# ScalarE and VectorE in source order: an attention and quantised-convolution kernel with its instruction order tied down on two engines

## Chip, cores and metric

The kernel runs on one core of one Trainium2 chip. The metric is the device time of one execution in microseconds (us). Five engines work side by side: TensorE (PE; its weight loads are PEld), ScalarE (ACT), VectorE (DVE), GpSimd (POOL) and SyncE (SP, which here only issues DMAs).

## What is computed

Input `x` is 16 images of 128 channels by 1024 pixels (32 x 32), all float32. First an attention layer with four heads, then two 3x3 convolutions on 4-bit activations with batch statistics. Cut to what matters:

```python
qkv = einsum('bchw,oc->bohw', x, w_qkv) + b_qkv            # 4 heads, 128 channels each
scores = einsum('bnc,bcm->bnm', q, k) * c ** -0.5           # 1024 x 1024 per image and head
out = einsum('bnm,bmc->bnc', softmax(scores), v)
x = einsum('bchw,oc->bohw', out, w_out) + b_out + x
# second layer: act_quant = round(15 * clip(x, 0, 1)) / 15, weights to 4 bits as well
out = conv3x3(act_quant(x), weight_quant(w1));  out = batchnorm(out, gamma1, beta1)
out = conv3x3(act_quant(out), weight_quant(w2)); out = batchnorm(out, gamma2, beta2)
return out + x
```

## The kernel before

Nearly all of the time is spent in one loop of `fast_path`. It goes over 63 of the 64 pairs of image and head (`heads`, index `g`; four heads, h = 0 to 3, belong to an image) and, inside a head, over `NK` = 4 steps `k`. The 64th pair (`LAST`) is done by a loop of its own (`score_unit`, `attend_unit`, `normalise_group`), which also starts the first convolution of the last image. The second convolution and the output follow in a second block that the change doesn't touch.

One step does this:

- `scores(g, k)`: TensorE makes four score chunks of 128 x 512, each as two instructions of 64 output rows (`halves`), which go to two halves of the array. I call these halves lanes. The chunks go to three PSUM buffers (`ps_s`, 3), so the fourth chunk of a step has to wait until the first has been read. ScalarE reads each chunk with an exponential into tile `e` (line 551). VectorE then forms the combinations that a Strassen-like scheme with seven products in place of eight needs: lines 554, 555 and 558 (the last one writes T4), and adds them into the running softmax sums `es` (562 in step 1, 564 in steps 2 and 3).
- `run(step, 0)`: work that was registered with `at` for the first half of the step.
- `attend(...)` of the step before: the seven products, each on one lane, into four PSUM banks `psa` (pool `ps_a`, one buffer each). In even steps four of the seven are on the first lane, in odd steps on the second. In an odd step the first product reads T4, and the last goes to bank 0.
- `run(step, 1)`: work registered for the second half.

The registered work of head `g` falls into the next head: `sum_up` (line 625) in its step 0, first half; `evacuate` (595, four copies of `psa` to SBUF on ScalarE) in step 0, second half; `combine` parts 0, 1 and 2 in step 1 (both halves) and step 2 (first half), which pass the result between ScalarE copies that move data to other partitions (605, 606, 607, 612, 615) and VectorE adds (608, 613, 617, 618); `normalise` in step 2, second half, which inverts the sums in a chain of small operations (652 to 660), spreads them (664) and applies them (673, or 675 and 676, and for the last head of an image also 679). With the last head of an image, `quantize` (255 on ScalarE, 256 and 257 on VectorE) and `sums_range` (348, 349) come in the first head of the next image, step 3; `transform_rows` (782) in the second head, step 0; `rows_product` (matmuls `psw`, ScalarE line 798) in steps 2 and 3 and the step after; `rows_output` (805, 806, 808) and `first_statistics` (298) in the third head, steps 0 and 1. The projections `project_u` (matmuls `psu`, ScalarE 509) for the next head come in steps 1 and 2, and `project_v` for the next image (matmuls `psv`, ScalarE copy 530, VectorE 532 and 533) in the last head of an image and the first of the next.

TensorE's order is written out by hand: `product` ties every matmul to the one before with `tc.issue_after`. The other engines' order is left to the scheduler of the framework. It takes the instructions in the order of the source as a priority, but puts one ahead of another where it reckons that the other would still be waiting. `tc.issue_after(x)` adds an edge of order without a semaphore: an instruction is placed behind `x` on its engine. Each engine then executes its own list.

```python
with tc.issue_after(pe[0]) if pe else nullcontext():
    done = nc.tensor.matmul(out_, lhsT=lhsT, rhs=rhs, start=start, stop=stop)
pe[:] = [done.ins]
```

Of the kernel before, what the change touches and what calls it, by code (L numbers as in the profile page):

```python
# [16 lines left out]
NH = 4  # L17
# [174 lines left out]
def fast_path(  # L192
# [29 lines left out]

    outer = ExitStack()
# [24 lines left out]
    def quantize(b, src, scale, bias, r0=0, r1=H):  # L248

        cut = slice(r0 * W, r1 * W)  # L250
        t = qtp.tile([P, (r1 - r0) * W], F32, tag="qt", name="qt")
        if b == B - 1 and scale == A_LEVELS and r1 == H:
            nc.vector.tensor_scalar(t, src[:, cut], scale, 0.0, ALU.mult, ALU.max)
        else:
            nc.scalar.activation(t, src[:, cut], AF.Relu, bias=bias, scale=scale)
        nc.vector.tensor_scalar(t, t, A_LEVELS, MAGIC, ALU.min, ALU.add)
        return nc.vector.tensor_scalar(
            pads[b % NPAD][:, r0 + 1 : r1 + 1, 1 : W + 1],
            t.rearrange("p (h w) -> p h w", w=W),
            MAGIC,  # L260
            None,
            ALU.subtract,
        )
# [82 lines left out]
    def sums_range(b):  # L346
        flat = sums[:, b * NH : (b + 1) * NH, :].rearrange("p g k -> p (g k)")
        nc.vector.tensor_reduce(ext[:, 0, b : b + 1], flat, AX.X, ALU.min)
        nc.vector.tensor_reduce(ext[:, 1, b : b + 1], flat, AX.X, ALU.max)
# [23 lines left out]
    with ExitStack() as ph:  # L373
# [86 lines left out]
        def fold_a(h):  # L460
            wq_h, wk_h, bq_h = wqk_sb[:, h, 0:P], wqk_sb[:, h, P : 2 * P], wqk_sb[:, h, 2 * P :]
            if h == 0:

                ps = ps_m.tile([P, P], F32, tag="mm", name=f"ps_a_{h}")
                bias = ps_a.tile([P, 1], F32, tag="a1", name="ps_a_bias")
            else:
                ps = ps_s.tile([P, P + 1], F32, tag="s", name=f"ps_a_{h}")
                bias = ps[:, P:]
            product(ps[:, 0:P], wq_h, wk_h)
            product(bias, wk_h, bq_h)  # L470
            nc.vector.tensor_scalar(at_sb[:, h, :], ps[:, 0:P], qscale, None, ALU.mult)
            nc.vector.tensor_scalar(au_sb[:, h : h + 1], bias, qscale, None, ALU.mult)

        def fold_b():
            ps = ps_m.tile([P, NH, P], F32, tag="mm", name="ps_b")
            for h in range(NH):
                product(ps[:, h, :], wvo_sb[:, h, 0:P], wvo_sb[:, h, P : 2 * P])
            nc.scalar.copy(bt_sb[:, 1, 1:], ps)
            nc.vector.tensor_copy(bt_sb[:, 1, 0], ps[:, NH - 1])
            nc.scalar.copy(bt_sb[:, 0, :, TOP], bt_sb[:, 1, :, TOP])  # L480
            nc.vector.tensor_tensor(
                bt_sb[:, 0, 0:NH, BOTTOM], bt_sb[:, 1, 0:NH, BOTTOM], bt_sb[:, 1, 0:NH, TOP], ALU.subtract
            )
            nc.vector.tensor_copy(bt_sb[:, 0, NH, BOTTOM], bt_sb[:, 1, NH, BOTTOM])

        def fold_bo():
            ps = ps_s.tile([P, 1], F32, tag="s", name="ps_bo")
            for h in range(NH):
                product(
                    ps,  # L490
                    wvo_sb[:, h, P : 2 * P],
                    wvo_sb[:, h, 2 * P :],
                    start=(h == 0),
                    stop=(h == NH - 1),
                )
            nc.vector.tensor_tensor(bo2_sb, ps, bo_sb, ALU.add)

        def project_u(g, hf, ps=None):
            b, h = heads[g]
            if hf == 0:  # L500
                us[g] = up.tile([P, N], F32, tag="u", name=f"u_{g}")
            if ps is None:
                ps = ps_m.tile([P, HALF], F32, tag="mm", name=f"psu_{g}_{hf}")
            halves(ps, lambda t: at_sb[:, h, LANES[t]], xt[b][:, ts(hf, HALF)])
            dst = us[g][:, ts(hf, HALF)]
            if g == 0 and hf == 0:
                nc.vector.tensor_scalar(dst, ps, au_sb[:, h : h + 1], None, ALU.add)
            else:
                copied = nc.scalar.activation(dst, ps, AF.Identity, bias=au_sb[:, h : h + 1])  # L509
                if g == 0:  # L510
                    load_rest(copied.ins)
# [8 lines left out]
        def project_v(b, k, c, ps=None):  # L520
# [9 lines left out]
            nc.scalar.copy(v[:, c : c + 3 : 2], ps.rearrange("p (h a o) -> p a h o", a=2, o=PH))  # L530
            if c == 1:
                nc.vector.tensor_tensor(v[:, S2], v[:, S3], v[:, A22], ALU.subtract)
                nc.vector.tensor_tensor(
                    v[:, S1 : S4 + 1],
                    v[:, A11 : A12 + 1],
                    v[:, S2 : S2 + 1].to_broadcast([P, 2, NH, PH]),
                    ALU.add,
                )
# [4 lines left out]
        def scores(g, k, between=None):  # L543
# [4 lines left out]
            for i, (c, m) in enumerate(((0, 1), (1, 1), (0, 0), (1, 0))):  # L548
                ps = ps_s.tile([P, HALF], F32, tag="s", name=f"pss_{g}_{k}_{i}")
                score(ps, b, g, k + NK * c, ts(m, HALF))  # L550
                exps[:] = [nc.scalar.activation(e[:, 2 * c + 1 - m], ps, AF.Exp).ins]  # L551
                if between and i in between:
                    between[i]()
            nc.vector.tensor_tensor(e[:, T3], e[:, B12], e[:, B22], ALU.add)  # L554
            nc.vector.tensor_tensor(  # L555
                e[:, T1 : T2 + 1 : T2 - T1], e[:, B12 : B11 + 1], e[:, B11 : T3 + 1 : T3 - B11], ALU.subtract
            )
            nc.vector.tensor_tensor(e[:, T4], e[:, T2], e[:, B21], ALU.add)  # L558
            mine = e[:, T4 : T3 + 1]
            if k == 1:  # L560
                sides[g] = esp.tile([P, NHF, HALF], F32, tag="es", name=f"es_{g}")
                nc.vector.tensor_tensor(sides[g], es[g, 0][:, T4 : T3 + 1], mine, ALU.add)  # L562
            elif k > 1:
                added = nc.vector.tensor_tensor(sides[g], sides[g], mine, ALU.add)  # L564
                sums_added[:] = [added.ins]
# [26 lines left out]
        def evacuate(g):  # L592
            evs[g] = [evp.tile([P, HALF], F32, tag=f"s{i}", name=f"ev_{g}_{i}") for i in range(4)]
            for to, ps in zip(evs[g], psa.pop(g)):
                nc.scalar.copy(to, ps)  # L595
# [5 lines left out]
        def combine(g, part):  # L601
            sa, sb, s3, sd = evs[g]
            if part == 0:
                y = avs[g, "y"] = evp.tile([P, HALF], F32, tag="y", name=f"y_{g}")
                nc.scalar.copy(y[TOP], s3[BOTTOM])
                nc.scalar.copy(y[BOTTOM], sd[TOP])  # L606
                nc.scalar.copy(sd[TOP], sd[BOTTOM])
                nc.vector.tensor_tensor(y, sa, y, ALU.add)  # L608
                return
            y = avs[g, "y"]  # L610
            if part == 1:
                nc.scalar.copy(s3[BOTTOM], y[TOP])
                nc.vector.tensor_tensor(y, y, s3, ALU.add)
            elif part == 2:
                nc.scalar.copy(sa[BOTTOM], y[BOTTOM])
                avs[g] = avp.tile([P, N], F32, tag="av", name=f"av_{g}")
                nc.vector.tensor_tensor(avs[g][:, HALF:], y, sd, ALU.add)
                nc.vector.tensor_tensor(avs[g][:, 0:HALF], sa, sb, ALU.add)
                evs.pop(g), avs.pop((g, "y"))

        def quadrant_sums(total):
# [3 lines left out]
            nc.vector.tensor_reduce(  # L625
# [11 lines left out]
        def inverse_sums(g, part, cut):  # L637
# [3 lines left out]
            if g == LAST:  # L641
# [5 lines left out]
                nc.vector.reciprocal(rinv, ps)  # L647
            else:

                side = smp.tile([Q, P // Q, n], F32, tag="side", name=f"side_{g}")  # L650
                for a in range(P // Q):
                    nc.vector.tensor_copy(side[:, a, :], part[ts(a, Q), :])
                total = smp.tile([Q, n], F32, tag="total", name=f"total_{g}")
                nc.vector.tensor_reduce(total, side.rearrange("p a k -> p k a"), AX.X, ALU.add)

                first, second = total[:, 0 : n // 2], total[:, n // 2 :]
                nc.vector.tensor_tensor(first, first, second, ALU.add)
                nc.vector.reciprocal(rinv[0:Q, :], total)
                for a in range(1, P // Q):
                    nc.vector.tensor_copy(rinv[ts(a, Q), :], rinv[0:Q, :])  # L660
# [3 lines left out]
            nc.vector.transpose(rb, rinv.unsqueeze(2).to_broadcast([P, n, Q]))  # L664
            return rb

        def normalise(g):
# [3 lines left out]
            if h == 0:  # L671
                accs[b] = accp.tile([P, N], F32, tag="acc", name=f"acc_{b}")
                nc.vector.tensor_tensor(accs[b], av, rb, ALU.mult)
                return
            nc.vector.tensor_tensor(av, av, rb, ALU.mult)  # L675
            nc.vector.tensor_tensor(accs[b], accs[b], av, ALU.add)
            if h == NH - 1 or g == LAST - 1:

                nc.vector.scalar_tensor_tensor(accs[b], accs[b], bo2_sb, xt[b], ALU.add, ALU.add)
# [15 lines left out]
        def score_unit(u):  # L695
# [9 lines left out]
            exps[:] = [nc.scalar.activation(e, ps, AF.Exp).ins]  # L705

        def attend_unit(u):
# [8 lines left out]
            elif u == FIRST_UNIT[i] + 1:  # L716
# [6 lines left out]
                nc.vector.tensor_tensor(totals[i], units[(u - 1) // 4][:, (u - 1) % 4], e, ALU.add)  # L723
            else:
                nc.vector.tensor_tensor(total, total, e, ALU.add)
# [15 lines left out]
            elif u + 1 == FIRST_UNIT[i + 1]:  # L741
# [3 lines left out]
                nc.scalar.copy(avs[LAST, i], psa[LAST, i])  # L745
                sides[LAST, i] = quadrant_sums(total)

        def normalise_group(i):
# [4 lines left out]
            nc.vector.tensor_tensor(rb, avs.pop((LAST, i)), rb, ALU.mult)  # L753
            nc.vector.tensor_tensor(x1[:, cut], x1[:, cut], rb, ALU.add)
# [15 lines left out]
        def transform_weights():  # L770
            with tc.issue_after(sums_added[0]):
                nc.vector.tensor_tensor(middle1[:, 1], taps1[:, 0], taps1[:, 2], ALU.add)
                nc.vector.tensor_tensor(middle1[:, 0], middle1[:, 1], taps1[:, 1], ALU.add)
                nc.vector.tensor_tensor(middle1[:, 1], middle1[:, 1], taps1[:, 1], ALU.subtract)

        def transform_rows(b):
# [3 lines left out]
            for k in (1, 2, 0, 3):  # L780
                x_, y_, op = FOUR[k]
                nc.vector.tensor_tensor(works[b][:, k], pick(x_), pick(y_), op)

        def rows_product(b, k):
# [13 lines left out]
            nc.scalar.mul(ms[b, inner][:, k // 2], ps, (1.0, 0.5, 0.5, -1.0)[k])  # L798

        def rows_output(b):  # L800
# [4 lines left out]
            nc.vector.tensor_tensor(both[:, 0], inner[:, 0], inner[:, 1], ALU.add)  # L805
            nc.vector.tensor_tensor(both[:, 1], inner[:, 0], inner[:, 1], ALU.subtract)
            y = ys[b].rearrange("p (i r w) -> p r i w", r=2, w=W)
            nc.vector.tensor_tensor(y, others, both, ALU.add)
# [541 lines left out]
```

## Time and profile before

| | |
|---|---|
| Time, median of 2 runs | 2024.68 us (2022.66 to 2026.7) |
| The profiled execution's own time | 2024.57 us |
| Its span in the profile | 2022.7 us, so 1.9 us lie around it |
| Mean granted TensorE clock | 0.993 |
| PE, DVE, ACT busy | 1987.6, 1722.2 and 1198.5 us |
| DMA | 22 GB/s in the mean |

The span is one profiled execution. A group line gives source line, engine, operation, output and input tiles, count, busy time, mean length of one, and the idle time of the engine just before, with what ended it. Times of a timeline are microseconds from the start of the span. A float32 matmul instruction shows as two entries in the profile, and a lane starts one entry after the other.

### The profile page before, as it was taken

What the parts mean: (1) busy time and instruction counts of PE and PEld (TensorE: products, weight loads), DVE (VectorE), ACT (ScalarE), POOL (GpSimd) and SP (SyncE); (2) the same over time, 40 slices, a digit from 0 to 9 for tenths busy, and PEclk for the clock granted to TensorE, in tenths of its full rate; (3) what the DMA queues carried; (4) which work ended last, traced back from release to release, by engine and by line L of the source; (5) the groups of instructions that cost most, each with busy time, mean ns of one, the idle gap of its engine ahead of it and who ended that gap; (6) DMA issues with size and microseconds to landing.
All of it is one profiled execution on the core that took longest, in us unless ns stands there. A gap on an engine that the chain in (4) does not pass through costs nothing. (4 is left out here: it accounts for less than half of the span.)

```text
span 2022.7 us, 24701 instructions
## 1 busy us (share of the span) xinstructions
PE 1987.6 (98%) x9497; PEld 730.3 (36%) x9497; DVE 1722.2 (85%) x2642; ACT 1198.5 (59%) x2007; POOL 19.7 (1%) x29
## 2 busy tenths in 40 slices
PE   9999999999999999999999999999999999999994
PEld 3543333333333333333333333433333333333441
DVE  5889888888888888888888888888888888878888
ACT  4565665665566566566556556656656655655575
POOL 0000000000000000000000000000000000000020
PEclk9999999999999999999999999999999999999997
DMA  1000000000000000000000000000000000000064
GB/s 42 24 1 22 1 22 1 22 0 1 22 1 22 1 9 14 0 22 1 21 1 1 22 1 21 11 22 11 1 22 11 22 11 21 11 1 11 11 239 168
DMA packets 12846, 43.74 MB, mean 22 GB/s; under 512 B 1456, under 2 KB 1840, under 8 KB 12720
## 3 DMA queue, kind: packets, MB, share of 16 engines
q1 hardware_dynamic: 9520, 32.05, 4.2%
q10 hardware_dynamic: 3200, 10.03, 1.5%
q8 instruction: 76, 1.25, 0.3%
q14 instruction: 50, 0.41, 0.1%
HBM read 22.16 MB, written 19.92 MB: 21 GB/s over the span
## 5 line engine op out<-in xcount | busy, mean ns | idle before, releaser
L403 PE MATMUL pss<-u,x 128*64 128x512 f32 (+1 forms) x4128 | 1031.9, 589 | 1.6 <-ACT u L509 1.6
L403 PE MATMUL psa<-e,vo 128*64 128x512 f32 (+1 forms) x3624 | 922.4, 588 | 0.0
L551 ACT ACTIVATE e<-pss 128x512 f32<-128x512 f32 x1008 | 595.4, 596 | 380.7 <-PE pss L403 331.9
L403 PEld LDWEIGHTS pss<-u,x 128*64 128x64 f32 x4128 | 351.6, 137 | 549.3 <-issue 493.4
L403 PEld LDWEIGHTS psa<-e,vo 128*64 128x64 f32 x3624 | 304.8, 137 | 483.5 <-issue 449.6
L555 DVE TENSOR_TENSOR e<-e 128x1024 f32<-128x1024 f32 x252 | 307.7, 1221 | 29.8 <-ACT e L551 21.6
L554 DVE TENSOR_TENSOR e<-e 128x512 f32<-128x512 f32 x252 | 172.2, 683 | 105.5 <-ACT e L551 101.7
L558 DVE TENSOR_TENSOR e<-e 128x512 f32<-128x512 f32 x252 | 174.0, 690 | 21.5 <-DVE e L555 0.5
L595 ACT COPY ev<-psa 128x512 f32<-128x512 f32 x252 | 135.5, 589 | 87.2 <-PE psa L403 87.0
L403 PE MATMUL psu<-x,at_sb 128*64 128x512 f32 x512 | 184.9, 599 | 1.0 <-DMA x<-in_x_dram 1.0
L403 PE MATMUL psv<-bt_sb,x 128*64 128x512 f32 x512 | 184.9, 592 | 1.0 <-ACT bt_sb L480 1.0
L530 ACT COPY vo<-psv 128x512 f32<-128x512 f32 x128 | 75.5, 590 | 142.3 <-PE psv L403 142.3
L564 DVE TENSOR_TENSOR es<-es,e 128x1024 f32<-128x1024 f32 x126 | 154.0, 1222 | 2.7
L509 ACT ACTIVATE u<-psu,au_sb 128x512 f32<-128x512 f32 x127 | 87.4, 688 | 21.7 <-PE psu L403 20.1
L798 ACT ACTIVATE m<-psw 128x512 f32<-128x512 f32 x60 | 35.9, 598 | 92.6 <-PE psw L403 90.7
L608 DVE TENSOR_TENSOR y<-ev,y 128x512 f32<-128x512 f32 x63 | 43.6, 692 | 52.4 <-ACT y L606 52.4
L664 DVE STREAM_TRANSPOSE rb<-sums 128x1024 f32<-128x1024 f32 (+1 forms) x66 | 79.8, 1210 | 1.6
L625 DVE TRANSPOSE_TENSOR_REDUCE part<-es 128x32 f32<-128x1024 f32 (+1 forms) x65 | 79.6, 1224 | 1.1
L403 PEld LDWEIGHTS psv<-bt_sb,x 128*64 128x64 f32 x512 | 53.6, 137 | 73.5 <-issue 66.7
L403 PEld LDWEIGHTS psu<-x,at_sb 128*64 128x64 f32 x512 | 53.5, 138 | 73.1 <-issue 69.1
L562 DVE TENSOR_TENSOR es<-e,e 128x1024 f32<-128x1024 f32 x63 | 76.8, 1219 | 0.0
L675 DVE TENSOR_TENSOR av<-av,rb 128x1024 f32<-128x1024 f32 x47 | 57.6, 1225 | 1.6
(159 smaller groups left out, 1193.6 us busy)
## 6 DMA issues: line engine op xcount, KB each, us to landing
x_dram<-acc SPq DMA_DIRECT2D x16, 512.0 KB, 4.3
x<-in_x_dram ACTq DMA_DIRECT2D x15, 512.0 KB, 4.6
res<-x_dram SPq DMA_DIRECT2D x1, 7680.0 KB, 30.0
y_dram<-y SPq DMA_DIRECT2D x6, 512.0 KB, 2.6
back<-y_dram SPq DMA_DIRECT2D x1, 3072.0 KB, 11.4
out_dram<-back SPq DMA_DIRECT2D x6, 512.0 KB, 4.5
out_dram<-y SPq DMA_DIRECT2D x5, 512.0 KB, 4.1
out_dram<-y SPq DMA_DIRECT2D x9, 256.0 KB, 2.5
```

Of the source, the lines that this page charges most:

```text
L403: done = nc.tensor.matmul(out_, lhsT=lhsT, rhs=rhs, start=start, stop=stop)
L509: copied = nc.scalar.activation(dst, ps, AF.Identity, bias=au_sb[:, h : h + 1])
L530: nc.scalar.copy(v[:, c : c + 3 : 2], ps.rearrange("p (h a o) -> p a h o", a=2, o=PH))
L551: exps[:] = [nc.scalar.activation(e[:, 2 * c + 1 - m], ps, AF.Exp).ins]
L554: nc.vector.tensor_tensor(e[:, T3], e[:, B12], e[:, B22], ALU.add)
L555: nc.vector.tensor_tensor(e[:, T1 : T2 + 1 : T2 - T1], e[:, B12 : B11 + 1], e[:, B11 : T3 + 1 : T3 - B11], ALU.subtract)
L558: nc.vector.tensor_tensor(e[:, T4], e[:, T2], e[:, B21], ALU.add)
L562: nc.vector.tensor_tensor(sides[g], es[g, 0][:, T4 : T3 + 1], mine, ALU.add)
L564: added = nc.vector.tensor_tensor(sides[g], sides[g], mine, ALU.add)
L595: nc.scalar.copy(to, ps)
L625: nc.vector.tensor_reduce(part, total.rearrange("p (k c) -> p k c", c=Q), AX.X, ALU.add, apply_transpose=True,)
L664: nc.vector.transpose(rb, rinv.unsqueeze(2).to_broadcast([P, n, Q]))
```

## The change

A small class wraps an engine. Every call through it is placed behind the call before it through the same wrapper, so all wrapped instructions of that engine stand in the order in which the source issues them. No semaphore and no arithmetic is added.

```diff
+    class InOrder:
+        def __init__(self, engine):
+            self.engine, self.last = engine, None
+
+        def __getattr__(self, name):
+            def call(*args, **kwargs):
+                with tc.issue_after(self.last) if self.last else nullcontext():
+                    done = getattr(self.engine, name)(*args, **kwargs)
+                self.last = done.ins
+                return done
+            return call
+
+    act, vec = InOrder(nc.scalar), InOrder(nc.vector)
...
-                exps[:] = [nc.scalar.activation(e[:, 2 * c + 1 - m], ps, AF.Exp).ins]
+                exps[:] = [act.activation(e[:, 2 * c + 1 - m], ps, AF.Exp).ins]
...
-            nc.vector.tensor_tensor(e[:, T3], e[:, B12], e[:, B22], ALU.add)
+            vec.tensor_tensor(e[:, T3], e[:, B12], e[:, B22], ALU.add)
...
             for to, ps in zip(evs[g], psa.pop(g)):
-                nc.scalar.copy(to, ps)
+                act.copy(to, ps)
...
             if part == 1:
-                nc.scalar.copy(s3[BOTTOM], y[TOP])
-                nc.vector.tensor_tensor(y, y, s3, ALU.add)
+                act.copy(s3[BOTTOM], y[TOP])
+                vec.tensor_tensor(y, y, s3, ALU.add)
```

In the same way `nc.scalar` becomes `act` and `nc.vector` becomes `vec` in `quantize`, `sums_range`, `fold_a`, `fold_b`, `fold_bo`, `project_u`, `project_v`, `scores`, `evacuate`, `combine`, `quadrant_sums`, `inverse_sums`, `normalise`, `score_unit`, `attend_unit`, `normalise_group`, `transform_weights`, `transform_rows`, `rows_product` and `rows_output`. Not wrapped are the DMAs, the statistics (298, 292), `gather`, the constants, the convolution weights (1249 to 1262), the ScalarE copies of the first convolution (293) and everything in the second block. The added lines stand ahead of line 223, so a line of the changed file is 17 higher than the same line before, and an instruction made through the wrapper carries line 232, that of the wrapper. The text uses the lines of the kernel before.

## The prediction

> **What bounds the kernel now.** First the table of busy time and the slices, then the costliest groups.
>
> ```profile
> PE 1987.6 (98%) x9497; PEld 730.3 (36%) x9497; DVE 1722.2 (85%) x2642; ACT 1198.5 (59%) x2007; POOL 19.7 (1%) x29
> ...
> PE   9999999999999999999999999999999999999994
> ...
> DVE  5889888888888888888888888888888888878888
> ACT  4565665665566566566556556656656655655575
> ...
> L551 ACT ACTIVATE e<-pss 128x512 f32<-128x512 f32 x1008 | 595.4, 596 | 380.7 <-PE pss L403 331.9
> ...
> L554 DVE TENSOR_TENSOR e<-e 128x512 f32<-128x512 f32 x252 | 172.2, 683 | 105.5 <-ACT e L551 101.7
> ```
>
> TensorE is busy throughout; ScalarE waits for TensorE and VectorE for ScalarE. A busy share doesn't say how full TensorE is, so I compare a period with its work, from the timeline (start, length, engine, line):
>
> ```profile
> 502.88 4.02 PE L403 MATMUL pss<-u,x 128*64 128x512 f32 x16
> ...
> 506.31 1.44 PE L403 MATMUL psu<-x,at_sb 128*64 128x512 f32 x4
> ...
> 507.17 3.17 PE L403 MATMUL psa<-e,vo 128*64 128x512 f32 x13
> ...
> 516.39 1.28 DVE L679 SCALAR_TENSOR_TENSOR acc<-acc,bo_sb,x 128x1024 f32<-128x1024 f32 x1
> ```
>
> Four chunks take 506.31 - 502.88 = 3.43 us, so a chunk is 0.86 and one product on one lane also 0.86. A projection (psu, psv) is 0.86. Seven products are 3.43 on the lane that has four, 2.57 on the other, 3.00 in the mean. Line 679, once an image, starts at 516.39 and again at 635.77: an image takes 119.38 us. Its matmuls: 16 steps x 6.43 + 8 psu x 0.86 + 8 psv x 0.86 + 4 psw x 0.64 (545.8 to 546.45 for one) = 119.1. TensorE has 0.3 us an image to spare; every wait that the change adds to it is added to the time.
>
> Such a wait is already there once, in head 1. ScalarE's timeline, then TensorE's:
>
> ```profile
> 53.33 0.59 ACT L595 COPY ev<-psa 128x512 f32<-128x512 f32 x1 [2.25 <-PE psa L403]
> 55.03 1.56 ACT L595 COPY ev<-psa 128x512 f32<-128x512 f32 x3 [1.11 <-PE psa L403]
> 56.47 1.12 ACT L551 ACTIVATE e<-pss 128x512 f32<-128x512 f32 x2
> ...
> 64.94 0.62 ACT L612 COPY ev<-y 64x512 f32<-64x512 f32 x1 [0.24 <-DVE y L608]
> ```
>
> ```profile
> 53.98 0.59 PE L403 MATMUL pss<-u,x 128*64 128x512 f32 x1
> ...
> 58.06 1.23 PE L403 MATMUL psu<-x,at_sb 128*64 128x512 f32 x4
> ```
>
> Three evacuations stand ahead of the first exponential; it ends at 57.1, the fourth chunk needs its buffer, and the chunks take 58.06 - 53.98 = 4.08 in place of 3.43. Copies follow each other every 0.48 (three in 1.56).
>
> **What the Trainium skill says.** "TensorE: Matmul & The Clock Gate", "Architectural detail: the array is 16× 32×32, not 1× 128×128": "ACT/DVE are strict FIFO". So what stands first and waits holds everything behind it; at 64.94 ScalarE sat 0.24 us for line 612's input with exponentials behind it, which fits. "TensorEngine Tiling (Array Packing)", "Key Properties": different tiles of the array run independently; here the two lanes' entries start in pairs, and one lane can be late while the other is not. The same page, "PSUM Bottleneck": tiling speeds up TensorE but not the evacuation of PSUM; the row above shows it. "Perfetto Trace Analysis", "Identifying the Most-Contended Engine": matmul busy share is a bad measure of headroom; hence my sum per image.
>
> **The change part by part.** It adds no arithmetic and no semaphore. TensorE's order stays except in the last microseconds; SP and POOL stay; ScalarE's loads of x come with line 255 as before. What moves is read from the order in the built program.
>
> *Evacuation (595).* Before: banks 1, 3, 0, 2, then the exponentials mixed with 605 to 607. Banks 1 and 3 close earlier: they were read from 501.36, the other two from 502.64. After: 0, 1, 2, 3, then four exponentials, then 605 to 607. Bank 0 closes last, so no copy starts before the products end. With T the start of the next step's chunks: products end at T + 0.16, first copy T + 0.20, first exponential after 4 x 0.48 at T + 2.12, its end (0.60) T + 2.72, fourth chunk about 0.11 later (56.47's exponential ended 0.1 before that chunk moved) at T + 2.83, against T + 2.57 unhindered. Loss 0.26 in a plain head. In the first head of an image a psv product follows the products and its copy (530) now stands ahead of the evacuations: copy at T + 0.20, exponential from T + 2.60, fourth chunk T + 3.31, loss 0.74. In the last head the psv product gives the copies 0.86 more: no loss.
>
> *The sums (652 to 679).* Before, 652 to 664 ran right after 625 in step 0 (625 at 527.11, 664 until 532.54). After, they stand where `normalise` is called: behind 618, ahead of line 554 of step 3. First head of an image, times from the start T2 of step 2's chunks on the first lane: the exponential that 554 needs ends at 3.4. Then VectorE has no gap: 554, 555, 558, 564 until 7.6 (4.1, as 573.9 to 578.0 in the timeline before), 617 and 618 +1.2, 652 to 660 +2.27 (528.39 to 530.66), 664 +1.28, 675 and 676 +2.5, 679 +1.3: 16.15. ScalarE stands at 255 (1.06) and can't take the next step's exponentials: first one 17.2 to 17.75, fourth chunk 17.9, unhindered 16.3. Then 554 to 558 of step 3 end at 18.9; step 3's products start with T4 and wait to 19.0 (unhindered 17.1). The lane with four products ends at 22.4 in place of 20.6: 1.8 late.
>
> *What follows in the second head.* VectorE still has no gap: 564 until 20.1, 256 and 257 +1.3, 348 and 349 +0.4, 554 to 558 +2.75, four of 782 +1.5, 625 +1.25, 554 to 558 +2.8, 562 +1.25, 608 +0.6: 31.8. Line 612 waits for 608 and the exponentials of step 2 stand behind 612: first one 32.4 to 32.9, fourth chunk 33.0. Unhindered it starts at 20.57 + 3.43 + 0.86 + 2.57 + 2.57 = 30.0. So this stretch loses 3.0 in all; the 1.8 above and this head's 0.26 are in it. Then the second head has no 679 and TensorE gets the psw products: VectorE catches up.
>
> *Third and fourth head.* Line 612 ends 0.4 to 0.5 before the exponential behind it could start, and T4 is 0.4 or more ahead of its product: no loss, but little room. Third head: evacuation 0.26.
>
> *Sum per image:* 3.0 + 0.26 + 0.74 = 4.0. Fifteen images have such a stretch: 60, less the 15 x 0.3 = 4 that TensorE lost before: +56.
>
> *Start.* 1252 (not wrapped) now stands right behind 1249 and waits for POOL until 58.23, where before 554 ran at 57.62: VectorE 1.2 late, and 612 ahead of an exponential: about 1.2 lost, twice (two weight sets): +2.
>
> *End.* The last adds (725 twice, 625, together 2.0) come behind the middle group's 257, the final sum matmul behind 16 convolution matmuls: +3 on the chain to the statistics. Bounds: 0 if cover is found, 5.
>
> *Costed at nothing:* the copy of bt_sb (480) now stands ahead of an exponential, and the first psv waited 1.0 for it, so up to 0.5 may come back; 615, 617 and 618 move to step 2, where the exponentials of that step and line 509 don't need them; 805 to 808 move behind 625, beside TensorE's step 0 products, and would cost at most their 2.6 once an image in a head with 0.4 to spare.
>
> Total: 2024.6 (the profiled execution) + 56 + 2 + 3 = 2086 (2085.6). The runs' median, 2024.7, is the same.
>
> **Rivals.**
> 1. *Not slower.* Place: first head, step 2 to 3. VectorE idles 15%, 17 us an image. If 679 ended by T2 + 14.5 in place of 16.15, and 608 in the next head by 30.2, exponentials would be in time and only small evacuation waits would replace those of today; the clean order (four exponentials together) would give back the 0.3 an image: 2024.6 - 4 = 2021. For it: the idle share. Against it: the sum is made of measured lengths without a gap. It decides if VectorE is 1.6 us faster there.
> 2. *Half absorbed.* Lanes take turns in being ahead by 0.86; a delay that hits the lane that is ahead may cost nothing. Then the stretch loses 3.0 - 0.86 = 2.1, less 0.5 if 555 to 564 overlap more, and evacuation 0.5: 2.1 x 15 - 4 + 3 = +31: 2056. Against it: the lane ahead has the four products next.
> 3. *It spreads.* The small room of third and fourth head is used up (0.45 each late), and the lanes stay out of step at evacuation, which costs up to 0.43 in three heads: 4.0 + 0.9 + 1.3 = 6.2; 93 - 4 + 5 = +94: 2119. For it: so little room. Against it: a late TensorE gives the others time.
>
> **How the numbers follow.** Forecast 0.70 (2066 to 2108), rival 3 0.11, rival 2 0.15, rival 1 0.04. The range for 8 in 10 is 2058 to 2112: the stretch at 2.0 in place of 3.0 gives 2071, without start and end 2066, and some of rival 2 and 3 are in it. A measurement of this kernel can tell about 2% (40 us) from no change; 2065 is that bound. Slower by over 2%: forecast 0.69, rival 3 0.11, together 0.80; within 2%: 0.19; faster by over 2%: 0.01, since TensorE has only 4 us to give back.
>
> **What would show it.** Right: an image takes 123.1 us between two of its adds of bias and x (679); the four chunks after an evacuation take 3.7 (plain) and 4.2 (first head) in place of 3.43; in the first head of an image ScalarE waits over 3 us for 679 ahead of 255, and in the second for 608 ahead of 612; VectorE has no gap from step 2 to there. Busy times stay, TensorE's share falls to about 96%. Wrong, if an image takes under 121 or over 125.5 us, if third and fourth head lose as much as the first two, or if the longest new TensorE gaps are at psa products that wait for T4.

## The result, and the profile after

The kernel after takes 2102.36 us (median of two runs, 2101.45 to 2103.27); the kernel before takes 2024.68. The ratio is 1.0384, 95% interval 1.0335 to 1.0432: slower, as forecast, and 16 us above the predicted 2086, inside the range. The profiled execution has a span of 2099.5 us (2022.7 before).

In the profile after, every wrapped instruction carries line 232, the line of the wrapper's call; other lines stand 17 higher than before (403 is 420). The text keeps the numbers of the kernel before. The page's first line and the two costliest TensorE groups, then the view of waits (engine, tile, line, releaser: total us, times, longest):

```profile
PE 2035.9 (97%) x9497; PEld 863.0 (41%) x9497; DVE 1744.8 (83%) x2642; ACT 1185.2 (56%) x2007; POOL 19.4 (1%) x29
...
L420 PE MATMUL pss<-u,x 128*64 128x512 f32 (+1 forms) x4128 | 1072.8, 592 | 20.0 <-ACT e L232 15.4
L420 PE MATMUL psa<-e,vo 128*64 128x512 f32 (+1 forms) x3624 | 924.8, 590 | 8.9 <-ACT e L232 7.8
```

```profile
PEld pss L420 <- ACT e L232: 115.6, 171, 2.4
...
ACT qt L232 <- DVE acc L232: 68.1, 17, 11.0
...
PEld psa L420 <- DVE e L232: 19.5, 34, 1.0
```

The first two of these waits in the kernel before:

```profile
PEld pss L403 <- ACT e L551: 17.8, 67, 0.7
ACT qt L255 <- DVE acc L679: 15.9, 15, 1.1
```

The instructions are the same in number, yet TensorE's busy time has grown by 48 us: the busy figure counts part of the stalls (and the half clock described below), and its share says little. The waits say more. The weight loads of score chunks waited for an exponential for 17.8 us in the kernel before, now 115.6. Line 255 (`qt`) waited 15.9 us for 679 in all, now 68.1, of which 51.8 are 14 visits in the middle of the run, 3.7 each. The waits of products for VectorE (`psa <- DVE e`, T4) are a sixth of those of the chunks.

Between two 679s an image takes 123.48 us in place of 119.38: +4.10. I call lateness the time by which an entry of TensorE starts later than the same entry in the kernel before. It is 0.8 us at 137 us, 62.3 in the last head before its one long gap, and 76.7 at the end of the convolutions: 15 x 4.10 = 61.5 in the images and 14.3 from that gap on. The spans of the two profiled executions differ by 76.8, the medians by 77.7. Over the four heads of an image the 4.10 splits into 1.13, 2.32, 0.62 and 0.04.

The stretch, in VectorE's timeline and then ScalarE's, for the image whose step 2 (first head) starts on TensorE at T2 = 525.06:

```profile
528.36 2.86 DVE L232 TENSOR_TENSOR e<-e 128x512 f32<-128x512 f32 x3
...
533.59 0.72 DVE L232 COPY side<-part 32x32 f32<-32x32 f32 x4
...
539.70 1.28 DVE L232 SCALAR_TENSOR_TENSOR acc<-acc,bo_sb,x 128x1024 f32<-128x1024 f32 x1
540.90 2.81 DVE L232 TENSOR_TENSOR e<-e 128x512 f32<-128x512 f32 x3
...
555.85 0.68 DVE L232 TENSOR_TENSOR y<-ev,y 128x512 f32<-128x512 f32 x1
557.22 0.69 DVE L232 TENSOR_TENSOR y<-y,ev 128x512 f32<-128x512 f32 x1 [0.69 <-ACT ev L232]
```

```profile
541.01 1.06 ACT L232 ACTIVATE qt<-acc 128x1024 f32<-128x1024 f32 x1 [3.70 <-DVE acc L232]
...
541.98 1.55 ACT L232 ACTIVATE e<-pss 128x512 f32<-128x512 f32 x3
...
547.50 2.05 ACT L232 COPY ev<-psa 128x512 f32<-128x512 f32 x4 [3.17 <-PE psa L420]
...
556.57 0.62 ACT L232 COPY ev<-y 64x512 f32<-64x512 f32 x1 [2.09 <-DVE y L232]
557.21 1.57 ACT L232 ACTIVATE e<-pss 128x512 f32<-128x512 f32 x3
```

VectorE has no bracket (no idle time) from 528.36 to the end of 608 at 556.53. Twice ScalarE stands still in front of an instruction that waits for VectorE, and both times a run of three exponentials follows at once: those chunks had been finished and were only queued behind. TensorE's timeline shows the first price: the fourth chunk waits for a buffer until the first of those exponentials has ended.

```profile
539.10 3.16 PE L420 MATMUL pss<-u,x 128*64 128x512 f32 x12
542.61 1.08 PE L420 MATMUL pss<-u,x 128*64 128x512 f32 x4 [0.35 <-ACT e L232]
```

### The profile page after: what moved, and what is told of

Same layout as the page of the kernel before. It is cut to its first block, busy times and chain, and to the rows that moved or that the text cites. A ratio compares the mean times of both kernels' runs of the same rounds, so it can differ in the third digit from the quotient of the medians.

```text
span 2099.5 us, 24657 instructions
## 1 busy us (share of the span) xinstructions
PE 2035.9 (97%) x9497; PEld 863.0 (41%) x9497; DVE 1744.8 (83%) x2642; ACT 1185.2 (56%) x2007; POOL 19.4 (1%) x29
## 5 line engine op out<-in xcount | busy, mean ns | idle before, releaser
L420 PE MATMUL pss<-u,x 128*64 128x512 f32 (+1 forms) x4128 | 1072.8, 592 | 20.0 <-ACT e L232 15.4
L232 DVE TENSOR_TENSOR e<-e 128x512 f32<-128x512 f32 x756 | 655.9, 868 | 193.8 <-ACT e L232 146.7
L420 PEld LDWEIGHTS pss<-u,x 128*64 128x64 f32 x4128 | 394.5, 137 | 542.2 <-issue 412.5
L420 PEld LDWEIGHTS psa<-e,vo 128*64 128x64 f32 x3624 | 345.6, 137 | 473.1 <-issue 435.7
L420 PE MATMUL psu<-x,at_sb 128*64 128x512 f32 x512 | 163.4, 593 | 0.3 <-DVE au_sb L232 0.3
L232 DVE TENSOR_TENSOR es<-es,e 128x1024 f32<-128x1024 f32 (+1 forms) x134 | 159.8, 1193 | 4.5
L232 DVE TENSOR_TENSOR vo<-vo 128x256 f32<-128x256 f32 (+1 forms) x128 | 71.3, 557 | 63.4 <-ACT vo L232 61.2
L232 ACT COPY ev<-y 64x512 f32<-64x512 f32 x126 | 77.7, 617 | 65.9 <-DVE y L232 63.9
L232 ACT COPY y<-ev 64x512 f32<-64x512 f32 x126 | 77.8, 618 | 3.1
L232 DVE TENSOR_TENSOR y<-y,ev 128x512 f32<-128x512 f32 x63 | 43.5, 691 | 31.9 <-ACT ev L232 31.8
```

The source lines that it names most:

```text
L232: done = getattr(self.engine, name)(*args, **kwargs)
```

## The experiments

Theory A is that of the prediction: the sums on VectorE come so late that ScalarE stands at 255 and 612 with exponentials behind (the stretch), and the evacuations hold exponentials up by themselves. Its rivals are in the expectations. "An image" is the period between two 679s.

### Only one engine in source order

```diff
-    act, vec = InOrder(nc.scalar), InOrder(nc.vector)
+    act, vec = InOrder(nc.scalar), nc.vector
```

> Only ScalarE keeps the order of the source; VectorE's is the scheduler's again, and in it 652 to 664 stand right behind 625 in step 0. Theory A (the stretch comes from the late sum chain on VectorE, the rest from the evacuations on ScalarE): the waits for 679 ahead of 255 and for 608 ahead of 612 are gone (under 1 us), the evacuation losses of about 0.9 (first head) and 0.7 (third head) remain, less the 0.3 that the kernel before lost anyway: an image takes 120.5 to 121.0 us, the end costs some 8: 2024.7 + 15 x 1.4 + 8 = 2054 (2044 to 2064). Rival B (any fixed order of ScalarE puts the exponentials behind 255 and 612, whatever VectorE does): an image near 123, 2085 or more. Rival C (the fixed order of ScalarE alone costs nothing): 2027 or less.

2064.07 us, ratio 1.0197 [1.018, 1.0214]; an image takes 121.52. In its view of waits, line 255's wait for 679 is down to 9.2 us in all, 6.9 of them in one visit:

```profile
ACT ev L232 <- DVE y L625: 12.6, 17, 3.3
ACT qt L232 <- DVE acc L771: 9.2, 2, 6.9
```

So with a free VectorE the two long waits are gone, and rivals B and C fall. But 2.14 an image is left where A put 1.1 to 1.6: ScalarE's own part was priced too low.

```diff
-    act, vec = InOrder(nc.scalar), InOrder(nc.vector)
+    act, vec = nc.scalar, InOrder(nc.vector)
```

> Only VectorE keeps the order of the source; the scheduler now puts the exponentials ahead of 612 and 255 where VectorE is late. Theory A: exponentials come in time, evacuations are as before, and what is left of the stretch is T4 of step 3 behind 679, about 1.8 late in the first head, less 0.3: an image takes 120.7 to 121.3 us, start and end cost 2 to 6: 2024.7 + 15 x 1.6 + 4 = 2053 (2040 to 2066). Rival C (the late VectorE alone sets the whole stretch; ScalarE's waits stand beside it): an image 122.3 or more, 2072 or more. Rival D (VectorE's lateness is harmless without ScalarE's waits): under 119.8, 2033 or less.

2134.74 us, ratio 1.054 [1.0523, 1.0558], an image 126.12: slower than with both orders fixed, a case that no expectation named. Rival C's number (122.3 or more) is met, but its reason can't be the whole: if the late VectorE alone set the stretch, this kernel would lose no more than the one with both orders fixed. TensorE's lateness now grows by 3.5, 1.4 and 1.7 us in the second, third and fourth head of an image (0.2 in the first). ScalarE's timeline in a third head (here 568 is 551, and 622, 623, 629, 632 are 605, 606, 612, 615):

```profile
593.49 0.62 ACT L622 COPY y<-ev 64x512 f32<-64x512 f32 x1
594.02 0.58 ACT L568 ACTIVATE e<-pss 128x512 f32<-128x512 f32 x1
594.63 0.62 ACT L623 COPY y<-ev 64x512 f32<-64x512 f32 x1
...
599.82 0.62 ACT L629 COPY ev<-y 64x512 f32<-64x512 f32 x1 [2.10 <-DVE y L232]
601.19 0.62 ACT L632 COPY ev<-y 64x512 f32<-64x512 f32 x1 [0.76 <-DVE y L232]
601.83 1.58 ACT L568 ACTIVATE e<-pss 128x512 f32<-128x512 f32 x3
```

The scheduler's ScalarE order suits a VectorE that does 608 as soon as 605 to 607 allow. It mixes these copies with the exponentials of step 1, and puts 612 and even 615 ahead of those of step 2. VectorE, tied to the source, first does 554 to 562 of that step, which need the last of the delayed exponentials, and only then 608. The next run tests this.

```diff
-                act.copy(y[TOP], s3[BOTTOM])
-                act.copy(y[BOTTOM], sd[TOP])
-                act.copy(sd[TOP], sd[BOTTOM])
+                with tc.issue_after(exps[0]):
+                    act.copy(y[TOP], s3[BOTTOM])
+                    act.copy(y[BOTTOM], sd[TOP])
+                    act.copy(sd[TOP], sd[BOTTOM])
```

> As vec_only (126.12 us an image), with the three copies 605 to 607 held behind the last exponential of their step, as the source has them; the rest of ScalarE is the scheduler's. Theory K (in vec_only these copies, mixed with the exponentials of step 1, delay the last one by up to 3 x 0.62; VectorE, which must do 554 to 562 before 608, is late with 608, and the exponentials of step 2 stand behind 612: about 1.6 lost in each of four heads): most of the 1.6 comes back in each head, an image takes 120.3 to 121.8 us, 2134.7 - 15 x 5 = 2060 (2050 to 2072). Rival L (it is the place that the scheduler gave to 255 and 612 themselves): 124 or more, 2104 or more.

One execution: 2095.33 us, an image 123.42. The copies account for 2.70 of the 6.74 lost an image, half of what theory K expected; L's figure isn't reached either. In ScalarE's timeline (630 and 633 are 612 and 615) the ping-pong of 612 and 615 with VectorE is still there, ahead of three exponentials:

```profile
584.25 0.62 ACT L630 COPY ev<-y 64x512 f32<-64x512 f32 x1 [0.69 <-DVE y L232]
585.63 0.61 ACT L633 COPY ev<-y 64x512 f32<-64x512 f32 x1 [0.76 <-DVE y L232]
586.27 1.57 ACT L568 ACTIVATE e<-pss 128x512 f32<-128x512 f32 x3
```

In source order 615 stands behind these exponentials. That it costs the rest, beside the late sums, is read from this view and was not tried by itself.

### The two parts of the theory, undone one by one

The sums early, for the fourth head of each image alone (`invert` calls `inverse_sums` and keeps its result for `normalise`; for the other heads it is registered right ahead of `normalise`, so their order stays):

```diff
             at(end, 0, sum_up, g)
+            if h == NH - 1:
+                at(end, 0, invert, g)
```

> All stays as in the kernel after, but in the first head of each image (the sums of the fourth head of the image before) 652 to 664 stand right behind 625 in step 0 in place of behind 618 in step 2; 675, 676 and 679 stay. Theory A: VectorE has the 3.55 us of the chain out of its gapless run, so 679 ends about 12.6 after T2 and 608 of the second head in time; the two long ScalarE waits fall under 1 us, the evacuation losses (0.9 and 0.7) stay: an image takes 120.7 to 121.2 us in place of 123.48, and the time is 2102.4 - 15 x 2.5 = 2064 (2056 to 2072). Rival E (the loss is a sum of many small displacements, 617, 618 and 805 to 808 too): an image 122.3 or more, 2085 or more.

2072.76 us, ratio 1.0233 [1.0216, 1.025], an image 121.42: 2.06 back, against 2.5 expected. Line 255's waits for 679 in the middle of the run go from 51.8 to 3.5 us (14 visits, from the rows of its tile), and 612 in the second head waits 0.81 in place of 2.09:

```profile
535.06 1.06 ACT L232 ACTIVATE qt<-acc 128x1024 f32<-128x1024 f32 x1 [0.22 <-DVE acc L232]
...
551.52 0.62 ACT L232 COPY ev<-y 64x512 f32<-64x512 f32 x1 [0.81 <-DVE y L232]
```

Rival E falls: moving one chain of eleven instructions takes half of the loss away. 1.84 of it comes back in the second head, 0.24 in the third.

The evacuations first:

```diff
-            for to, ps in zip(evs[g], psa.pop(g)):
-                act.copy(to, ps)
+            banks = psa.pop(g)
+            for i in (1, 3, 2, 0):
+                act.copy(evs[g][i], banks[i])
...
+        for g in range(LAST):
+            at((g + 1) * NK, 1, evacuate, g)
         for g in range(LAST):
...
-            at(end, 1, evacuate, g)
```

> All stays as in the kernel after, but the four evacuations are issued in the order of banks 1, 3, 2, 0 (1 and 3 close before the products end) and ahead of the psv copy of the same half step. Theory A: the fourth chunk of the first and third head is no longer late, 0.87 and 0.7 come back: an image takes 121.9 to 122.4 us, 2102.4 - 15 x 1.4 = 2081 (2075 to 2088). Rival F (the evacuation losses are swallowed by VectorE's lateness that follows; taking them away only lengthens the next wait): an image 123.2 or more, 2098 or more.

2070.98 us, ratio 1.0227 [1.021, 1.0244], an image 121.58: 1.90 back, more than the 1.4 expected, and rival F falls. ScalarE in the first head of an image, in the kernel after and then in this one:

```profile
516.63 0.59 ACT L232 COPY vo<-psv 128x512 f32<-128x512 f32 x1 [2.94 <-PE psv L420]
517.11 2.06 ACT L232 COPY ev<-psa 128x512 f32<-128x512 f32 x4
519.02 1.63 ACT L232 ACTIVATE e<-pss 128x512 f32<-128x512 f32 x3
```

```profile
510.52 1.56 ACT L232 COPY ev<-psa 128x512 f32<-128x512 f32 x3 [0.18 <-PE psa L420]
512.24 0.59 ACT L232 COPY vo<-psv 128x512 f32<-128x512 f32 x1 [0.15 <-PE psv L420]
513.15 0.60 ACT L232 ACTIVATE e<-pss 128x512 f32<-128x512 f32 x1 [0.32 <-PE pss L420]
```

Above, ScalarE sits 2.94 us before the `psv` copy, then four evacuations and the exponentials follow without a gap, so these are late. Below, each exponential waits for its chunk: ScalarE is ahead again. By heads, 1.05 comes back in the first, 0.23 in the second and 0.60 in the third. Which half of the edit does it?

> As the kernel after, with the evacuations in the order of banks 1, 3, 2, 0, but behind the psv copy as before that edit. Theory A: it helps the heads without a psv copy (two copies run before the products end), about 0.7 an image; in the first head the psv copy still holds all four: an image takes 122.5 to 122.9 us, 2102.4 - 15 x 0.75 = 2091. Rival M (the whole 1.90 of evac_first is the bank order): 121.7 or less, 2076. Rival N (it is all the place ahead of the psv copy): 123.3 or more, 2100.

One execution with the bank order alone (the first of the two hunks): 2094.13 us, an image 123.10. It gives 0.38; the place ahead of the `psv` copy gives the other 1.52. Both theories of one cause (M, N) miss, and A's 0.6 to 1.0 for the banks was too much. The bank order does clear the third head (0.02 in place of 0.62), but the loss of the first grows from 1.13 to 1.37. The place alone was not run, so the split holds only for undoing the two in this order.

The same edit with VectorE left to the scheduler (the edits of act_only and evac_first):

> As act_only (121.52 us an image), with the evacuations as in evac_first. Theory A (what a fixed ScalarE order costs while VectorE is free is the evacuations alone): an image takes 119.4 to 119.9 us, 2064.1 - 15 x 1.9 = 2035 (2028 to 2042). Rival O (part of the 2.14 is 605 to 607 behind all four exponentials, or the exponentials behind 612): 120.4 or more, 2047 or more.

One execution: 2036.5 us, an image 119.90. So 1.62 of act_only's 2.14 are the evacuations. Of the 0.52 that stay, 0.43 lie in the second head. There the scheduler's VectorE order puts that head's sum chain ahead of 608 (626 here), 612 waits for 608, and three exponentials follow at once:

```profile
539.30 0.62 ACT L232 COPY ev<-y 64x512 f32<-64x512 f32 x1 [1.66 <-DVE y L626]
539.94 1.58 ACT L232 ACTIVATE e<-pss 128x512 f32<-128x512 f32 x3
```

This is rival O's second guess, at half of the size that it gave. It is read from the view and was not undone by itself.

### The end

```diff
+    free = []
...
-                with tc.issue_after(self.last) if self.last else nullcontext():
+                with tc.issue_after(self.last) if self.last and not free else nullcontext():
...
+        free.append(True)
         n_units, lag, next_ = 2 * NCH, 4, 0
```

> As the kernel after, but from the last head on (behind the 63rd) the scheduler places ScalarE's and VectorE's instructions again. Theory A: the 15 images stay at 123.48 us each; what TensorE loses in the last head (its delay against the kernel before grows by 14.8 us there, 8.2 of it one gap before a psa product and the rest 605, 606 and 615 behind exponentials that come one by one) comes back: 2102.4 - 12 = 2090 (2087 to 2094). Rival G (most of the 14.8 is only an older lateness of VectorE that shows up at the end, or a fixed cost of the clock): 2096 or more.

2087.95 us, ratio 1.0317 [1.03, 1.0334], the images unchanged at 123.48: 14.4 back, and rival G falls. The last head in the kernel after, ScalarE and TensorE:

```profile
1992.11 0.63 ACT L232 ACTIVATE qt<-acc 128x512 f32<-128x512 f32 x1 [11.02 <-DVE acc L232]
1992.64 1.07 ACT L232 ACTIVATE e<-pss 128x512 f32<-128x512 f32 x2
```

```profile
1984.43 1.03 PE L420 MATMUL pss<-u,x 128*64 128x256 f32 x8
1993.27 1.98 PE L420 MATMUL psa<-e,vo 128*64 128x256 f32 x8 [7.81 <-ACT e L232]
```

ScalarE stands 11.02 us at the first group's quantisation, with the exponentials of the next score units behind it; TensorE runs out of both buffers and products. In end_free the scheduler puts those exponentials first, and `qt` starts without a wait. The table by stretches (us, busy and count of PE, PEld, DVE, ACT, POOL, then the granted clock, DMA share and GB/s), first of after, then of end_free:

```profile
1984.00:1998.00 14.00, 6.19 (x36) 3.38 (x34) 11.20 (x18) 3.34 (x7) 0.00 (x0) 0.64 0.00 0
```

```profile
1984.00:1998.00 14.00, 14.00 (x112) 8.76 (x109) 10.80 (x27) 6.40 (x13) 0.00 (x0) 1.00 0.30 115
```

The clock column holds a second cost: after the gap TensorE gets half of its clock, and eight entries of 128x256 take 1.98 in place of 1.03. A third cost stands at the last sum matmuls (`psr`). In the kernel after they come behind 17 convolution matmuls, in the kernel before right behind the products:

```profile
2000.78 2.93 PE L299 MATMUL psc<-pad,wq 128*128 128x480 bf16 x17
2003.91 0.61 PE L420 MATMUL psr<-part,quad 128*128 128x8 f32 x4 [0.21 <-DVE part L232]
```

```profile
1926.18 1.95 PE L403 MATMUL psa<-e,vo 128*64 128x256 f32 x16
1928.06 0.61 PE L403 MATMUL psr<-part,quad 128*128 128x8 f32 x4
```

TensorE's lateness goes from 62.3 to 70.3 over the gap, to 72.7 by the last product under the half clock, and to 75.9 at the last of these sum matmuls: 8.0, 2.4 and 3.1 us. The remaining 0.8 come in the convolutions behind, where another gap (2.56 us) is followed by 3.4 us at half of the clock. In end_free all three are gone.

### All three edits, and doses

> The edits of evac_first, chain_early and end_free together, the order otherwise that of the source. Theory A: the losses add, since evac_first gave 1.90 and chain_early 2.06 of the 4.10 us an image: an image takes 119.4 to 119.7 us, and with start and end the time is 2024.7 + 15 x 0.15 + 3 = 2030 (2024 to 2037). Rival H (both edits removed the same loss, the rest comes from elsewhere): an image 120.5 or more, 2043 or more.

2025.63 us, ratio 1.0006 [0.9999, 1.0013], an image 119.48. The losses add: 4.10 - 2.06 - 1.90 = 0.14 expected from the parts, 0.10 measured. The source's order on both engines is as fast as the scheduler's, once two groups of instructions are issued elsewhere in the source and the last head is left to the scheduler.

The doses are two more adds of 128x512 (0.688 us each; VectorE's busy time grows by 1.32 us an image) in step 2:

```diff
                 added = vec.tensor_tensor(sides[g], sides[g], mine, ALU.add)
                 sums_added[:] = [added.ins]
+                for _ in range(2 if k == 2 and h == 0 and g > 3 else 0):
+                    vec.tensor_tensor(spare, e[:, B12], e[:, B22], ALU.add)
```

> As the kernel after, with two more adds of 128x512 into an unread tile on VectorE (1.3 us together) in step 2 of the first head of each image, ahead of 617, 618 and the sum chain. Theory A (VectorE is without a gap from there to 608 of the second head, and that end releases ScalarE and TensorE): every microsecond is on the path, an image takes 124.6 to 124.8 us in place of 123.48, the time is 2102.4 + 15 x 1.2 = 2120. Rival I (VectorE, 83% busy, swallows it; the losses are ScalarE's evacuations): under 123.8, 2107 or less.

> The same two adds, but in step 2 of the second head, behind the stretch. Theory A: VectorE catches up there beside TensorE's psw products, so that little is lost: an image takes 123.5 to 123.9 us, 2102 to 2108. Rival J (it is VectorE's total load that counts, wherever it lies): 124.6 or more, 2119.

One execution each: in the first head (h == 0) an image takes 124.80 us, +1.32, in the second (h == 1) 123.47, no change; the times are 2126.16 and 2102.3. (The first rose by 23.8, 4 more than 15 x 1.32: this execution began 1.9 later, and two of its images, at 125.7, have 3.4 us of half clock in them.) The same work on the same engine costs all of its length in one head and nothing in the next. Rivals I and J fall, and VectorE's gapless run is shown to be what sets the end of the stretch.

Last, all_three with `invert` behind `sum_up` in every head (`if h == NH - 1` taken away):

> As all_three, with the sum chain 652 to 664 right behind 625 in every head. If VectorE has room for it in step 0 of the other heads: an image takes 119.1 to 119.5 us in place of 119.48, the time is 2023 (2019 to 2027). If it makes T4 of step 0 late there: 119.9 or more, 2031 or more.

2128.9 us, ratio 1.051 [1.0488, 1.0532], most images 125.9: 6.4 worse than all_three. By heads that is 2.2 in the second and 4.2 in the third; the fourth loses nothing. VectorE and ScalarE in its second head:

```profile
553.86 1.49 DVE L234 TENSOR_TENSOR rows<-pad 128x544 bf16<-128x544 bf16 x4
...
556.55 0.72 DVE L234 COPY side<-part 32x32 f32<-32x32 f32 x4
```

```profile
564.70 0.62 ACT L234 COPY ev<-y 64x512 f32<-64x512 f32 x1 [3.47 <-DVE y L234]
565.34 1.57 ACT L234 ACTIVATE e<-pss 128x512 f32<-128x512 f32 x3
```

Here 782 and 625 fill step 0 already; the sums on top make 608 late, and 612 keeps the exponentials waiting 3.47 us. In the third head 805 to 808 stand between the sums and 608, 612 waits 3.75 us, and TensorE gets a gap (ScalarE, then TensorE):

```profile
597.32 0.62 ACT L234 COPY ev<-y 64x512 f32<-64x512 f32 x1 [3.75 <-DVE y L234]
```

```profile
598.61 1.36 PE L422 MATMUL pss<-u,x 128*64 128x512 f32 x4 [2.20 <-ACT e L234]
```

The gap is again paid twice, as the stretch with the gap and the one behind it show (columns as in the table above):

```profile
595.90:599.30 3.40, 1.20 (x7) 0.34 (x6) 2.30 (x4) 1.96 (x4) 0.00 (x0) 1.00 0.00 0
599.30:602.70 3.40, 3.40 (x10) 0.98 (x8) 3.16 (x4) 2.13 (x4) 0.00 (x0) 0.50 0.00 0
```

Two images of this run have no half clock in them and take 124.21; so 1.7 of the 6.4 are the clock. The place that cures the first head harms the second and third.

## Why the prediction was right, and where its sum was off

- *The lane to follow.* TensorE full, every wait added to it: right. Doses and parts add up to a few hundredths of a microsecond an image.
- *The stretch's timetable.* From T2 = 525.06, forecast and measured: 679 ends at 16.15 / 15.92; the exponentials behind 255 start at 17.2 / 16.92; the next fourth chunk 17.9 / 17.55 (unhindered 16.3; 16.31 in the kernel before); 608 ends at 31.8 / 31.47; the exponentials behind 612 start at 32.4 / 32.15; fourth chunk 33.0 / 32.80 (unhindered 30.0; 30.05 before). A sum of measured lengths without a gap held for 32 us to within 0.35 (its items for the second head add up to 31.95, not 31.8).
- *The split of the 4.0 an image.* The sum came out at 4.10, its two terms did not. The stretch's 3.0 had the second head's evacuation (0.26) in it, so 2.74 was forecast for the late sums and 1.26 for all evacuations; chain_early gave 2.06 back and evac_first 1.90. The cut between them was wrong: with the sums early, the fourth chunk that was compared with "unhindered 30.0" still comes at 31.11, and in that run's ScalarE timeline the second head's four evacuations and three exponentials stand ahead of it without a gap. Two errors of 0.7 cancelled; that the sum came so close is luck.
- *Evacuation.* In the first head the fourth chunk comes 3.39 after the first of its step, 3.31 was forecast. In the second and third head it comes 3.71 and 3.62 after it, where 2.83 was forecast: the copies start 1.1 and 1.0 after the chunks (547.50 against 546.39 in the second head), and the working had put them at 0.20, though its own lines of head 1 have three of them at 55.03 and the chunks at 53.98. Most of what came back is the place ahead of the `psv` copy (1.52 of 1.90), the bank order only 0.38.
- *The 0.3 an image of the kernel before* were taken off as if the fixed order gave them back. Act_evac and all_three, at 119.90 and 119.48, do not beat 119.38: nothing came back. That is 15 x 0.3 = 4 us of the miss. (The prediction's own items for an image's matmuls add up to 119.2, not 119.1, so the room was 0.2.)
- *Start.* In the second and third head of the run, where the weight sets are, TensorE's lateness grows by 3.1 us (2 forecast), and by 3.0 in end_free. In this execution the first loads had landed earlier and TensorE was 2.6 ahead before, so only 0.5 of it is in the time.
- *End.* The step that failed: +3, bounds 0 to 5, measured +14.3. What it named came as it said: the last sum matmul behind the convolution matmuls, 3.1. But the working looked only at VectorE's last adds and TensorE's last matmul, and never asked what stands behind 255 of the first group on ScalarE, the very question that it had asked for each image. That wait cost 8.0 as a gap and 2.4 by the half clock behind it, and the working has neither. 11 of the 16 us between 2086 and 2102 lie here.
- *Rivals.* 1 falls by the result, and the doses show that the stretch has no slack. Rival 2 would have had the fourth chunk 2.1 late at the end of the stretch; it is 2.75 late (32.80 against 30.05). That chain_early gave 2.06 back does not speak for it, since the rest is evacuation and not absorbed. Rival 3's sign is there in the third head (0.62 against 0.26), its size is not, and the fourth head loses 0.04.
- *Tests named ahead.* 123.1 us an image (123.48); 255 over 3 us (3.70); 612 over 3 us (2.09 here: the exponentials before it had come late too, so it started its wait later); the first two heads lose 3.4 of the 4.1, the last two 0.7; the four chunks after an evacuation, up to the next matmul, take 4.3 in the first head (4.2 forecast), but 4.6 and 4.5 in the second and third (3.7 forecast); new gaps at chunks and not at T4's products (115.6 against 19.5 us of waits); TensorE's share 96% (97%, since busy time grew).

## What to carry to other kernels

On engines that execute a list in order, price a fixed order by what stands behind each instruction that waits for another engine, and do so in each stage, the last one too. Orders of two engines belong together: one that suits a partner's old order can be worse than both fixed. Before work is moved to a place where it helps, look whether each turn of the loop has room there; a dose of known length at that place tells in one run. Where a wait leaves TensorE a gap of 2 us or more, look at the granted clock behind it.

## What the runs showed of the hardware

The half clock at the end was not expected. In the kernel after, no matmul is shown between 1985.46 and 1993.27, and the granted clock is half from 1987.8 to 1998.0, 10.2 us, though TensorE worked again for the last 4.7 of these. The Trainium skill, "TensorE: Matmul & The Clock Gate", Part 1 ("The HAM clock gate"), gives windows of about 3.4 us and a return to full speed after a busy one; 10.2 is three such windows, which agrees. That page puts the throttle after an idle window; here it began 2.3 us after the last matmul's modelled end, and in all_heads after a gap of only 2.20 us, in a window that matmuls filled to 1.20 of 3.40 us. So a window need not be idle.

The traces of the fourteen kernels bound it further. Inside a trace all changes of the clock lie whole multiples of 3.413 us apart. Cut on that grid, every window of full clock that was followed by half clock was filled by matmuls to 49% or less, and every one that was followed by full clock to 42% or more; where between these the border lies they don't tell. Half clock ended after windows filled to 98% or more, and went on after one of 94%. The ends of matmuls are modelled, so these shares are estimates. A window of half clock, 3.4 us, cost 1.7 us in all_heads (125.90 against 124.21 an image) and 0.9 in dose_h0 (125.7 against 124.8).
